# A graph network's last graph layer: 65-column matmuls become 32-column tiles, and in layer 0 the early sums move ahead of the bias rows

## The chip, the cores and the metric

The kernel runs on one core of one Trainium2 chip. The metric is the device time in microseconds of one execution. A core has a matrix engine (TensorE, with a queue for weight loads and one for matmuls), VectorE, ScalarE, GpSimd (POOL) and a queue for transfers (SyncE), which run side by side and wait for each other at semaphores. Each engine takes its own instructions in the order in which they stand, so one that waits holds up all that stand behind it on its engine.

## The reference, cut to what matters

The network has 3125 nodes of 256 features and 100,000 edges, and four layers. Each layer normalizes the rows, adds the results of a graph part and of a mixing part (attention without a softmax over pairs) to `x`, and then adds a feed-forward part with experts:

```python
edge_index = jnp.stack([src, dst])
xn = _layernorm(x, axis=-1)
x = x + _L0_gnn_ref(xn, edge_index, ...) + _L0_mix_ref(xn[None], ...)[0]
x = x + _L0_ffn_ref(_layernorm(x, axis=-1)[None], ...)[0]
...
xn = _layernorm(x, axis=-1)
x = x + _L3_gnn_ref(xn, edge_index, L3_gnn_W, L3_gnn_att_src, L3_gnn_att_dst) + _L3_mix_ref(xn[None], ...)[0]
x = x + _L3_ffn_ref(_layernorm(x, axis=-1)[None], ...)[0]
```

Two parts are touched by the change. The graph part of the last layer is graph attention with four heads of 64 channels:

```python
xp = (x @ W).reshape(n, 4, 64)
a_src = jnp.einsum('nhc,hc->nh', xp, att_src)
a_dst = jnp.einsum('nhc,hc->nh', xp, att_dst)
e = jax.nn.leaky_relu(a_src[src] + a_dst[dst], 0.2)
e_exp = jnp.exp(e - e_max[dst])
denom = jax.ops.segment_sum(e_exp, dst, num_segments=n)
alpha = e_exp / denom[dst]
out = jax.ops.segment_sum(alpha[:, :, None] * xp[src], dst, num_segments=n)   # then relu
```

The feed-forward part of layer 0 sends each node to two of 16 experts:

```python
topk_vals, topk_idx = jax.lax.top_k(x @ gate_w + gate_b, 2)
topk_w = jax.nn.softmax(topk_vals, axis=-1)
expert_out = relu(x @ w1 + b1) @ w2 + b2          # per expert
y = x + jnp.sum(topk_w[..., None] * sel, axis=2)  # sel: the two chosen outputs
return layernorm(y) * gamma + beta
```

Layer 2's graph part weights messages by `edge_weight`; for it the kernel needs sums of the edge weights by source node, which depend on no layer and are computed early.

## The kernel before, in words

**Layout.** Nodes lie as 25 blocks (`NB`) of 125 (`P`) rows: `self.x` and `self.xn` are [125, 25, 256], `self.xt` is the normalized matrix transposed. Work over nodes goes in seven `PIECES` of up to 500 columns (`PW`): six of 500 and one of 125. All matmuls named here are float32. `self.bank()` gives one of four rotating accumulators of the matrix engine's output memory (PSUM[...]); `evac` (L159) copies an accumulator out, on VectorE and ScalarE in turn.

**The order of work.** The program is traced in Python, and a scheduler places each engine's instructions at build time by priority, which follows the order of tracing, and by its own estimate of times. The code shapes it by the order in which it traces, by generators that yield their progress (`together`, L1905, always advances the one that is behind), by an edge that keeps instructions behind a given one (`issue_after`), and by the number of buffers of each tile.

**The last graph layer (`l3_gnn_mix`, L1837; `l3_dense`, L1915).** The attention over edges is done densely: the number of edges from source block b to target piece p is stored in DRAM as bf16 (`ctt_d`), and the exponential of the leaky relu is written as a product of a source factor and a target factor plus a relu. `xr` [125, 25, 4, 65] holds the features by source block and head with a 65th column of ones, so the same matmul that sums the messages also sums the weights (`denom`). The pieces are taken two by two (three groups of 1000 targets, then one of 125), the heads two by two, except in the last group, which does four at once. For each of these turns there are 25 steps, one a source block b:

- SyncE loads the adjacency rows `cs` (two transfers by `move`, three buffers);
- for each head of the turn ScalarE makes `t` (L1965), VectorE makes `z = (t + u) * cs` (L1968, three buffers), 125 x 1000;
- TensorE adds into one accumulator for each head and piece, with 65 columns of weights (L1971):

```python
nc.tensor.matmul(acc[h, k][:, :w], xr[:, b, k4, :], z[:, k * PW:k * PW + w],
                 start=(b == 0), stop=(b == NB - 1))
```

Four accumulators live through a turn. At its end they are evacuated into `at`, a part of `self.xn` that is free in this stage, transposed back by blocks of 125 targets (L1987), and `finish` (L1923) divides by the sum, applies the relu and adds to `x`: five small VectorE operations for each block. `target_rows` loads the target factors `rows` of the next group. In the same stage runs the mixing part by pieces (`l3_mix_by_pieces`, L2005), paced at 1.15 to 1.0, and behind every finished piece the router of the last feed-forward part (`follow` in `l3_ffn`), with its scatter of rows `bx_d` by POOL (L2255).

**Layer 0's feed-forward part (`l0_ffn`, L1050).** VectorE works out a slot for every node and choice; POOL scatters the rows of `self.xn` into DRAM by 50 indirect transfers (L1117). `add_rows` adds `beta` to `x` (L982), and `times_rows` (L285) adds the experts' second biases, weighted by the gates, onto `self.xn`, into which the experts' outputs are gathered later: for each piece a transpose of the gates (L291), an evacuation, and for each block a matmul (L297) and an addition on VectorE (L298). Since this addition writes a block of `self.xn` that the scatter reads, it waits for that block's two transfers. Then come the first quarter (`EARLY = 0.25`) of the sums of edge weights (`weights_by_source`, L509), kept behind the instruction `placed`, which makes the slots:

```python
with tc.issue_after(placed.ins):
    for part in sums:
        if part > EARLY:
            break
```

A group of these sums is five VectorE operations (L537, L539, three at L543, each with three buffers) and four bf16 matmuls (L545). After them the 26 expert tiles follow: load of the rows `xb`, transposes (L1156), copies `xbt` on VectorE (L1158), the first matmul (L261), relu, the second matmul (L1168), and a further share of the sums with each tile.

Of the kernel before, what the change touches and what calls it, by code (L numbers as in the profile page):

```python
# [12 lines left out]
F32 = mybir.dt.float32  # L13
# [4 lines left out]
AF = mybir.ActivationFunctionType  # L18
OP = mybir.AluOpType
# [4 lines left out]
N = 3125  # L24
D = 256
P = 125
NB = 25
# [10 lines left out]
PW = 500  # L38
# [52 lines left out]
def _tables():  # L91
# [12 lines left out]
    t[NT1 * 128:NT1 * 128 + NB, 0] = np.arange(NB) * P  # L104
    return np.ascontiguousarray(t.reshape(NT1 + 1, 128, 4).transpose(1, 2, 0))
EARLY = 0.25
PIECES = [(i, min(PW, N - i)) for i in range(0, N, PW)]


class Net:  # L110
    NE, TS = 16, 384
# [938 lines left out]
    def l0_ffn(self, fast=False):  # L1050

        nc, tc, a = self.nc, self.tc, self.a
        NE, TS, ST, NT, bx = self.NE, self.TS, self.TS // 128, self.NT, self.bx
        by = self.dram.tile([NT * TS, D], F32, name="b0y_d")
        with ExitStack() as s:
            sb = s.enter_context(self.pool("f0_sb"))
            wk = s.enter_context(self.pool("f0_wk", 2))
            b2 = sb.tile([NE, D], F32, name="b2")
            nc.scalar.dma_start(b2, a["L0_ffn_b2"])
            gamma = self.load_b(sb, "L0_ffn_gamma")  # L1060
            beta = self.load_b(sb, "L0_ffn_beta")
            g, w, i8 = self.top2(sb, None, NE, P, NB, self.greatest)
# [17 lines left out]
            for e in range(NE):  # L1080
                nc.vector.tensor_tensor_scan(run[:, :, e], self.ones[:, :NB], tot[:, :, e], 0.0,
                                             op0=OP.mult, op1=OP.add)
# [4 lines left out]
                                    op0=OP.mult)  # L1087
# [15 lines left out]
            own = sb.tile([1, NT], I32, name="own")  # L1103
# [11 lines left out]
            for b in range(NB):  # L1115
                for j in range(2):
                    st = nc.gpsimd.indirect_dma_start(  # L1117
                        out=bx, out_offset=bass.IndirectOffsetOnAxis(ap=slot[:, j, b:b + 1], axis=0),
                        in_=self.xn[:, b, :], in_offset=None, bounds_check=NT * TS - 1, oob_is_err=False)
                    tc.declare_no_dep(st.ins, group="slots", reason="each choice has a slot of its own")  # L1120
                    tc.add_to_no_dep_group("slots", st.ins)
            self.add_rows(beta)
            y = self.xn
            self.times_rows(sb, g, b2, NE, y, self.xn)
            with ExitStack() as s2:
                sums = None
                if fast:
                    sums = self.weights_by_source(s2.enter_context(self.pool("w_sb")),
                                                  s2.enter_context(self.pool("w_wk", 3)), self.bank())

                    with tc.issue_after(placed.ins):
                        for part in sums:
                            if part > EARLY:
                                break
                wk2 = s2.enter_context(self.pool("f0_t", 3))
                pl = s2.enter_context(self.pool("f0_ps", 4, space=PSUM))
                s2.enter_context(tc.manual_schedule(engines={mybir.EngineType.SP}))
# [4 lines left out]
                for i in range(NT):  # L1142
# [10 lines left out]
                    for h in range(HB):  # L1153
                        ps = bank()
# [5 lines left out]
                    for f in range(4):  # L1160
                        ps = bank()
# [675 lines left out]
    def l3_gnn_mix(self, before, arrivals):  # L1837
# [6 lines left out]
        with ExitStack() as s:  # L1844
# [9 lines left out]
            sb = s.enter_context(self.pool("g3_sb"))  # L1854
            wk = s.enter_context(self.pool("g3_wk", 2))
            pa = s.enter_context(self.pool("g3_ps", 1, space=PSUM))
            xr = sb.tile([P, NB, 4, 65], F32, name="xr")
            nc.gpsimd.memset(xr[:, :, :, 64:65], 1.0)
            al = sb.tile([P, NB, 8], F32, name="al")
            for b in range(NB):  # L1860
                ps = self.bank()
                self.mm_tok(ps[:P, :264], self.xt, b, wx)
                nc.vector.tensor_copy(xr[:, b, :, :64], ps[:P, :D].rearrange("p (h d) -> p h d", h=4))
                nc.scalar.copy(al[:, b, :], ps[:P, 256:264])
            m = sb.tile([P, 8], F32, name="m")
            nc.vector.tensor_reduce(m, al.rearrange("p b h -> p h b"), axis=AX.X, op=OP.max)
# [47 lines left out]

    def l3_dense(self, sb, wk, pa, xr, us, r_d):  # L1915

        nc = self.nc
        few = sb.tile([P, NB, 4], F32, name="few")
        free = self.xn.rearrange("p b d -> p (b d)")
        rows = free[:, :8 * PW].rearrange("p (h d) -> p h d", h=4)  # L1920
        at = free[:65, 8 * PW:12 * PW].rearrange("p (h d) -> p h d", h=2)

        def finish(b, h0, nh, acc):  # L1923

            nc.vector.tensor_scalar(few[:, b, h0:h0 + nh], acc[:, :, 64], 1e-20, None, op0=OP.is_lt)
            rd = wk.tile([P, 4], F32, name="rd")
            nc.vector.tensor_scalar(rd[:, :nh], acc[:, :, 64], 1e-20, None, op0=OP.max)
            nc.vector.reciprocal(rd[:, :nh], rd[:, :nh])
            t = wk.tile([P, 4, 64], F32, name="tf")
            nc.vector.tensor_mul(t[:, :nh], acc[:, :, :64], rd[:, :nh, None].to_broadcast([P, nh, 64]))  # L1930
            v = self.x[:, b, h0 * 64:(h0 + nh) * 64]
            nc.vector.scalar_tensor_tensor(v, t[:, :nh].rearrange("p h d -> p (h d)"), 0.0, v,
                                           op0=OP.max, op1=OP.add)

        def target_rows(i, h0):

            n = min(2 * PW, N - i)
            for h in (h0, h0 + 1):
                if n > 0:
                    self.move(nc.sync, rows[:P, h, :n], r_d[h, i:i + n].partition_broadcast(P))  # L1940

        done, there = 0, []
        for h0 in (0, 2):
            target_rows(0, h0)
        for p0 in range(0, len(PIECES), 2):
            pcs = PIECES[p0:p0 + 2]
            n = sum(w for _, w in pcs)
            hg = 4 if n < PW else 2
            for h0 in range(0, 4, hg):
                acc = {}  # L1950
                for h in range(hg):
                    for k in range(len(pcs)):
                        acc[h, k] = pa.tile([65, 512], F32, name=f"acc{h * len(pcs) + k}")
                for b in range(NB):
                    cs = wk.tile([P, 2, PW], BF, name="cs", bufs=3)
                    if len(pcs) == 2:
                        self.move(nc.sync, cs, self.ctt_d[p0:p0 + 2, :, b, :].rearrange("k p d -> p k d"))
                        c = cs.rearrange("p k d -> p (k d)")
                    else:
                        self.move(nc.sync, cs[:, 0, :n], self.ctt_d[p0, :, b, :n])  # L1960
                        c = cs[:, 0, :n]
                    for h in range(hg):
                        k4 = h0 + h
                        t = wk.tile([P, 2 * PW], F32, name="t5")
                        nc.scalar.activation(t[:, :n], rows[:, k4, :n], AF.Relu, bias=us[:, 2, b, k4:k4 + 1],  # L1965
                                             scale=us[:, 0, b, k4:k4 + 1])
                        z = wk.tile([P, 2 * PW], F32, name="z", bufs=3)
                        nc.vector.scalar_tensor_tensor(z[:, :n], t[:, :n], us[:, 1, b, k4:k4 + 1], c,  # L1968
                                                       op0=OP.add, op1=OP.mult)
                        for k, (i, w) in enumerate(pcs):  # L1970
                            nc.tensor.matmul(acc[h, k][:, :w], xr[:, b, k4, :], z[:, k * PW:k * PW + w],  # L1971
                                             start=(b == 0), stop=(b == NB - 1))
                        done += n
                    yield done / (NB * N * 4)
                    if b == 5:
                        for i in there:
                            self.arrive(i)
                        there = []
                if hg == 2:
                    target_rows(pcs[0][0] + 2 * PW, h0)  # L1980
                    for h in range(2):
                        for k, (i, w) in enumerate(pcs):
                            self.evac(at[:, h, k * PW:k * PW + w], acc[h, k][:, :w])
                    for j in range(n // P):
                        ps = self.bank()
                        for h in range(2):
                            nc.tensor.transpose(ps[:P, h * 65:(h + 1) * 65], at[:, h, j * P:(j + 1) * P],  # L1987
                                                self.ident[:65, :65])
                        finish(p0 * 4 + j, h0, 2, ps[:P, :130].rearrange("p (h c) -> p h c", h=2))
                        yield done / (NB * N * 4)  # L1990
                else:
                    for h in range(4):
                        self.evac(at[:, h // 2, h % 2 * P:(h % 2 + 1) * P], acc[h, 0][:, :P])
                    ps = self.bank()
                    for h in range(4):
                        nc.tensor.transpose(ps[:P, h * 65:(h + 1) * 65], at[:, h // 2, h % 2 * P:(h % 2 + 1) * P],
                                            self.ident[:65, :65])
                    finish(p0 * 4, 0, 4, ps[:P, :260].rearrange("p (h c) -> p h c", h=4))

            there = [i for i, w in pcs]  # L2000
        for i in there:
            self.arrive(i)
        nc.vector.tensor_reduce(self.viol[:P, 5:6], few.rearrange("p b h -> p (b h)"), axis=AX.X, op=OP.add)
# [421 lines left out]
```

## Time and profile before

| | |
|---|---|
| Time, median of 3 runs | 4813.85 us (4810.83 to 4815.78) |
| The profiled execution's own time | 4666.18 us |
| Its span | 4664.4 us |
| TensorE clock granted, mean | 0.869 |
| TensorE busy | 3722.3 us (80%) |
| VectorE busy | 2505.6 us (54%) |
| ScalarE busy | 1302.8 us (28%) |
| POOL busy | 1020.2 us (22%) |
| Dense loop of the last graph layer | about 3530 to 4395 us of the span |
| Slots, scatter and early sums of layer 0 | about 796 to 926 us |

The profile is of one execution, with 50,401 instructions; its own time is 147.7 us below the median of the timed runs. A group of instructions is given as source line, engine, operation, the tile it writes and those it reads, shape and count, then busy time, mean duration in ns, idle time of the engine just before them, and what ended that idle time. PE is TensorE's matmul queue and PEld its weight loads; DVE is VectorE, ACT ScalarE. Durations of matmuls overlap, since they are pipelined; the distance of their starts tells what one costs. A float32 matmul shows as two records, each with a weight load of its own.

### The profile page before, as it was taken

The numbers are of one execution on the slowest core, as the hardware profiler recorded it, in microseconds if no ns is written. First come the engines' busy times: TensorE is split into PE (matmuls) and PEld (weight loads), VectorE is DVE, ScalarE is ACT, GpSimd is POOL, SyncE is SP. The second block draws the span as 40 slices with busy tenths as digits, with TensorE's granted clock in tenths as the row PEclk, the third lists the DMA queues.
The fourth block names the chain that finished last, engine by engine and source line by source line (L and its number), as shares of the span: only waits on it lengthen the run. The fifth ranks groups of instructions, "written<-read, shape, count | busy, mean of one in ns | idle before, by whom it ended". The sixth has DMA issues, their size and how long they took to land. (4 is left out here: it accounts for less than half of the span.)

```text
span 4664.4 us, 50401 instructions
## 1 busy us (share of the span) xinstructions
PE 3722.3 (80%) x16695; PEld 2505.9 (54%) x16695; DVE 2505.6 (54%) x8604; ACT 1302.8 (28%) x2336; POOL 1020.2 (22%) x1041
## 2 busy tenths in 40 slices
PE   1887796499938799999656566766799999999698
PEld 0676695277724556555545455655464444444466
DVE  5877317544475526994322323444265666777544
ACT  1367100022213223323100000000155655555521
POOL 2000000400055000000577777775000000000011
PEclk9786896599959799999877777887899999999699
DMA  6244630244332000000333333334102222221232
GB/s 176 75 113 118 138 82 22 81 135 140 107 85 40 4 29 9 13 14 7 106 105 106 104 104 104 104 104 139 58 7 59 59 63 56 63 52 49 74 107 68
DMA packets 256035, 358.86 MB, mean 77 GB/s; under 512 B 62719, under 2 KB 199350, under 8 KB 255765
## 3 DMA queue, kind: packets, MB, share of 16 engines
q1 hardware_dynamic: 135900, 176.07, 13.1%
q0 software_dynamic: 62832, 126.93, 10.3%
q10 hardware_dynamic: 57033, 52.54, 4.2%
q8 instruction: 136, 2.23, 0.2%
q14 instruction: 134, 1.10, 0.1%
HBM read 268.73 MB, written 94.97 MB: 78 GB/s over the span
## 5 line engine op out<-in xcount | busy, mean ns | idle before, releaser
L1601 POOL DMA_INDIRECT hg<-hx_d,idx x782 | 743.3, 950 | 282.8 <-issue 214.2
L1617 PE MATMUL acc<-hg,to 128*125 128x256 f32 x2042 | 584.5, 449 | 197.9 <-DVE to L1612 192.8
L1617 PEld LDWEIGHTS acc<-hg,to 128*125 128x125 f32 x2042 | 455.4, 227 | 309.3 <-DVE to L1612 216.3
L1971 PE MATMUL acc<-z,xr 125*65 125x500 f32 (+1 forms) x1400 | 577.4, 556 | 14.3 <-DVE z L1968 13.0
L1965 ACT ACTIVATE t<-xn,us 125x1000 f32<-125x1000 f32 (+1 forms) x400 | 409.4, 1037 | 239.0 <-DVE z L1968 228.1
L1968 DVE SCALAR_TENSOR_TENSOR z<-t,us,cs 125x1000 f32<-125x1000 f32 (+1 forms) x400 | 409.3, 1028 | 115.5 <-PE acc L1971 92.6
L1971 PEld LDWEIGHTS acc<-z,xr 125*65 125x65 f32 x1400 | 188.9, 145 | 314.8 <-issue 265.5
L1605 DVE TENSOR_TENSOR kw<-hg,awt 128x8 f32<-128x8 f32 x98 | 16.4, 168 | 581.2 <-DMA hg<-hx_d,idx 513.2
L261 PE MATMUL ps<-xt,w 128*128 128x500 f32 (+1 forms) x672 | 269.0, 547 | 1.8 <-DMA w<-in_L_ffn_W_dram 1.8
L1612 DVE TENSOR_SCALAR to<-iota_w,rel_b,kw 128x125 f32<-128x125 f32 (+1 forms) x782 | 245.2, 383 | 35.6 <-PE acc L1617 28.7
L1536 DVE SCALAR_TENSOR_TENSOR junk<-iota_w,rel_b,lock 128x125 f32<-128x125 f32 (+1 forms) x782 | 248.1, 386 | 0.0
L2255 POOL DMA_INDIRECT bx_d<-row,slot x25 | 31.2, 1248 | 891.3 <-ACT t L1965 422.9
L589 PE MATMUL ps<-y,cb 125*125 125x256 bf16 x1875 | 214.7, 279 | 0.0
L589 PEld LDWEIGHTS <-cb 125*125 125x125 bf16 x1875 | 213.5, 141 | 0.1
L797 ACT ACTIVATE k<-k 125x128 f32<-125x128 f32 x50 | 15.9, 318 | 687.0 <-DVE k L796 686.9
L190 ACT ACTIVATE rstd_t<-rstd_t 125x4 f32<-125x4 f32 (+2 forms) x86 | 17.2, 203 | 645.8 <-DVE rstd_t L189 630.2
L255 PE MATMUL ps<-wo,h 128*125 128x256 f32 x800 | 187.7, 386 | 3.6 <-ACT h L1439 2.6
L243 PE MATMUL ps<-ident,xn 125*128 125x125 f32 x300 | 58.8, 347 | 159.8 <-DVE xn L209 159.7
L1445 DVE SCALAR_TENSOR_TENSOR x<-ps,lg,x 125x256 f32<-125x256 f32 x200 | 92.7, 480 | 173.6 <-PE ps L255 173.6
L261 PEld LDWEIGHTS ps<-xt,w 128*128 128x128 f32 x672 | 122.7, 193 | 114.7 <-issue 102.4
L261 PE MATMUL ps<-h,w 128*128 128x500 f32 (+1 forms) x448 | 179.5, 541 | 2.3 <-ACT h L1434 1.6
L255 PEld LDWEIGHTS ps<-wo,h 128*125 128x125 f32 x800 | 142.9, 187 | 65.9 <-ACT h L1439 43.7
(566 smaller groups left out, 6326.7 us busy)
## 6 DMA issues: line engine op xcount, KB each, us to landing
cs<-ctt_d SPq DMA_DIRECT2D x150, 218.8 KB
w<-in_L_ffn_w_dram SPq DMA_DIRECT2D x52, 512.0 KB
cnt_d<-cd SPq DMA_DIRECT2D x25, 683.6 KB
cb<-cnt_d SPq DMA_DIRECT2D x25, 683.6 KB
ctt_d<-ct ACTq DMA_DIRECT2D x6, 2734.4 KB
hg<-hx_d,idx POOLq DMA_INDIRECT x782, 2.8
b0x_d<-zero SPq DMA_DIRECT2D x1, 9984.0 KB
xb<-b0x_d SPq DMA_DIRECT2D x26, 384.0 KB
```

The lines of the kernel that those rows point to most:

```text
L243: self.nc.tensor.transpose(ps[:, j * P:(j + 1) * P], src[:, i // P + j, h * 128:(h + 1) * 128], self.ident[:P, :P])
L255: self.nc.tensor.matmul(ps, xt[:, h, b * P:(b + 1) * P], w[:, h, :], start=(h == 0), stop=(h == k - 1))
L261: self.nc.tensor.matmul(ps, w[:, h, :], xt[:, h, i:i + n], start=(h == 0), stop=(h == k - 1))
L589: nc.tensor.matmul(ps[:P, :D], cf[k][:, h * P:(h + 1) * P], y3[:, b0 + k, j, :], start=(k == 0 and j == 0), stop=(k == m - 1 and j == 2))
L1445: nc.vector.scalar_tensor_tensor(self.x[:, b, :], ps[:P, :D], g[:, b, e:e + 1], self.x[:, b, :], op0=OP.mult, op1=OP.add)
L1536: nc.vector.scalar_tensor_tensor(junk[:, :m * P], self.iota_w[:, :m * P], rel[:, c:c + 1], lock[:, b:b + m].rearrange("p b n -> p (b n)"), ...
L1601: nc.gpsimd.indirect_dma_start(out=hg[:, j, :], out_offset=None, in_=hx, in_offset=bass.IndirectOffsetOnAxis(ap=idx[:, c0 + j:c0 + j + 1], ...
L1612: nc.vector.tensor_scalar(to, self.iota_w[:, :nb * P], rel[:, c:c + 1], kw[:, j:j + 1], op0=OP.is_equal, op1=OP.mult)
L1617: nc.tensor.matmul(acc[k], to[:, (k - b) * P:(k - b + 1) * P], hg[:, j, :D], start=(c == first[k]), stop=(c == last[k]))
L1965: nc.scalar.activation(t[:, :n], rows[:, k4, :n], AF.Relu, bias=us[:, 2, b, k4:k4 + 1], scale=us[:, 0, b, k4:k4 + 1])
L1968: nc.vector.scalar_tensor_tensor(z[:, :n], t[:, :n], us[:, 1, b, k4:k4 + 1], c, op0=OP.add, op1=OP.mult)
L1971: nc.tensor.matmul(acc[h, k][:, :w], xr[:, b, k4, :], z[:, k * PW:k * PW + w], start=(b == 0), stop=(b == NB - 1))
```

## The change

It has two parts, which do not touch each other.

In `l3_dense`, `xr` loses its column of ones. A step's four 65-column matmuls become twelve of 32 columns: for each of the two `units` (a piece; in the last group a pair of heads) two heads with two halves of 32 channels each, written to the four column tiles (`tile_position=(0, q)`, q = 0, 32, 64, 96) of that unit's accumulator, and four more with 32 columns of ones, whose 32 equal result rows are the sums of the weights, for both units in a third accumulator. Three accumulators live through a turn, of four names taken in rotation. `z` has four buffers instead of three, and `t` lies in two fixed places of `self.xn`, where `at` lay. Each matmul is tied in order behind the one before it and behind both `z` of its step, with a raised priority; at every third step (`BURST`) the tie to the matmul before is kept and one is added to an instruction of other TensorE work that was the latest three bursts (`LAG`) earlier. The end of a turn evacuates three accumulators, transposes the sums once and the results by units, and works on up to four blocks at a time.

In `l0_ffn`, `add_rows` and `times_rows` are traced after the early sums instead of before them.

```diff
+BURST, LAG = 3, 3
...
-            self.add_rows(beta)
             y = self.xn
-            self.times_rows(sb, g, b2, NE, y, self.xn)
             with ExitStack() as s2:
...
                         for part in sums:
                             if part > EARLY:
                                 break
+                self.add_rows(beta)
+                self.times_rows(sb, g, b2, NE, y, self.xn)
                 wk2 = s2.enter_context(self.pool("f0_t", 3))
...
-            xr = sb.tile([P, NB, 4, 65], F32, name="xr")
-            nc.gpsimd.memset(xr[:, :, :, 64:65], 1.0)
+            xr = sb.tile([P, NB, 4, 64], F32, name="xr")
...
-                        for k, (i, w) in enumerate(pcs):
-                            nc.tensor.matmul(acc[h, k][:, :w], xr[:, b, k4, :], z[:, k * PW:k * PW + w],
-                                             start=(b == 0), stop=(b == NB - 1))
...
+                acc = [pa.tile([128, 512], F32, name=f"acc{(turn + j) % 4}") for j in range(3)]
...
+                        t = spare[h % 2]
...
+                        z = zs[h] = wk.tile([P, 2 * PW], F32, name="z", bufs=4)
...
+                    if steps % BURST == 0:
+                        marks.append(next((i for i in reversed(nc.cur_bb.bb.instructions)
+                                           if i.engine == mybir.EngineType.PE and i.name not in own), None))
+                        if len(marks) > LAG and marks[-1 - LAG] is not None:
+                            made.append(marks[-1 - LAG])
+                    steps += 1
+                    with self.tc.high_priority(600):
+                        for out, left, h0, j, k, w, q in (
+                                [(acc[u], xr[:, b, h0 + j, f:f + 32], h0, j, k, w, 64 * j + f)
+                                 for u, (h0, k, w) in enumerate(units) for j in range(2) for f in (0, 32)]
+                                + [(acc[2], self.ones[:P, :32], h0, j, k, w, 64 * u + 32 * j)
+                                   for u, (h0, k, w) in enumerate(units) for j in range(2)]):
+                            mm = nc.tensor.matmul(out[q:q + 32, :w], left, zs[h0 + j][:, k * PW:k * PW + w],
+                                                  start=(b == 0), stop=(b == NB - 1), tile_position=(0, q))
+                            for i in made:
+                                self.tc.add_manual_dep(mm.ins, i.name, row, reason="in one row")
+                            made = [mm.ins]
+                            own.add(mm.ins.name)
...
-                    for j in range(n // P):
-                        ps = self.bank()
-                        for h in range(2):
-                            nc.tensor.transpose(ps[:P, h * 65:(h + 1) * 65], at[:, h, j * P:(j + 1) * P],
-                                                self.ident[:65, :65])
-                        finish(p0 * 4 + j, h0, 2, ps[:P, :130].rearrange("p (h c) -> p h c", h=2))
...
+                finish(b0, pcs[0][1] // P, hs[0], 2 * len(hs), acc)
```

The new `finish`:

```python
        def finish(b, nb, h0, nh, acc):
            w, nu = nb * P, len(acc) - 1
            at = wk.tile([128, 3, PW], F32, name="at", bufs=1)
            for k in range(nu + 1):
                self.evac(at[:, k, :w], acc[k][:, :w])
            ps = self.bank()
            for j in range(nb):
                nc.tensor.transpose(ps[:P, j * 128:(j + 1) * 128], at[:, nu, j * P:(j + 1) * P], self.ident)
            sums = ps[:P, :nb * 128].rearrange("p (j q r) -> p j q r", j=nb, r=32)[:, :, :, 0]
            ...
            for k in range(nu):
                bk, hk = (b + 4 * k, h0) if nh == 2 else (b, 2 * k)
                ...
                for j in range(nb):
                    nc.tensor.transpose(ps[:P, j * 128:(j + 1) * 128], at[:, k, j * P:(j + 1) * P], self.ident)
                t = wk.tile([P, 4, 2, 64], F32, name="tf")
                nc.vector.tensor_mul(t[:, :nb], ...)
                ...
                nc.vector.scalar_tensor_tensor(v, t[:, :nb].rearrange("p j h d -> p j (h d)"), 0.0, v,
                                               op0=OP.max, op1=OP.add)
```

## The prediction

> **What bounds the kernel now.** I read three things in this order: the page's costliest groups, the busy time by stretch over the last graph layer, and the timeline there; then the timeline of layer 0 around its scatter. (The chain that ended last is followed back over only 6% of the span and says nothing of either place.) The groups of the page:
>
> ```profile
> L1971 PE MATMUL acc<-z,xr 125*65 125x500 f32 (+1 forms) x1400 | 577.4, 556 | 14.3 <-DVE z L1968 13.0
> L1965 ACT ACTIVATE t<-xn,us 125x1000 f32<-125x1000 f32 (+1 forms) x400 | 409.4, 1037 | 239.0 <-DVE z L1968 228.1
> L1968 DVE SCALAR_TENSOR_TENSOR z<-t,us,cs 125x1000 f32<-125x1000 f32 (+1 forms) x400 | 409.3, 1028 | 115.5 <-PE acc L1971 92.6
> ```
>
> TensorE idles 14.3 us ahead of its 1400 records, VectorE waits 92.6 us for TensorE and ScalarE 228.1 us for VectorE: the queue of waits ends at TensorE. The 700 float32 matmuls of the code are 1400 records, two to a matmul. Busy time of the stage's two parts (PE, PEld, DVE, ACT, POOL, then clock, DMA share and GB/s):
>
> ```profile
> 3530.00:4313.00 783.00, 770.94 (x2343) 340.66 (x2342) 544.57 (x1053) 460.55 (x514) 20.47 (x16) 0.99 0.21 57
> 4313.00:4395.00 82.00, 64.50 (x287) 42.86 (x285) 54.55 (x241) 53.96 (x117) 9.54 (x8) 0.69 0.12 26
> ```
>
> For 783 us TensorE is the bound (98%, granted clock 0.99) with VectorE at 70%. In the last 82 us, the 125-wide group, it isn't. The timeline of TensorE gives the true price of a record:
>
> ```profile
> 3699.51 8.55 PE L1971 MATMUL acc<-z,xr 125*65 125x500 f32 x20
> 3707.89 1.97 PE L1321 MATMUL ps<-bd,q_e 128*125 128x132 f32 x16
> ```
>
> Twenty starts in 8.38 us: 0.419 us apart. The mean of all, from their starts, is 0.416; I use 0.4175, so a matmul of 500 columns costs 0.835 us. A step of the loop (one source block, two heads, two pieces) is 4 of them, 3.34 us, against VectorE's 2 x 1.25 = 2.5 us and ScalarE's 2 x 1.22 = 2.44 us. 150 such steps are 501 us of the 783; about 282 us are the mix and the router.
>
> In layer 0:
>
> ```profile
> 808.71 3.04 POOL L1117 DMA_INDIRECT b0x_d<-xn,slot  x1 [32.71 <-DVE slot L1114]
> 815.96 0.42 DVE L298 TENSOR_TENSOR xn<-ps,xn 125x256 f32<-125x256 f32 x1 [5.31 <-DMA b0x_d<-xn,slot]
> 889.47 0.42 DVE L298 TENSOR_TENSOR xn<-ps,xn 125x256 f32<-125x256 f32 x1 [1.83 <-DMA b0x_d<-xn,slot]
> 892.92 0.47 PE L1156 MATMUL pl<-ident,xb 128*128 128x128 f32 x1 [1.02 <-DMA xb<-b0x_d]
> 926.19 0.56 DVE L1158 COPY xbt<-pl 128x384 f32<-128x384 f32 x1
> 926.80 1.65 PE L261 MATMUL pl<-xbt,w 128*128 128x384 f32 x2
> ```
>
> The 25 additions of L298 each wait for two scatters, 54 us in all, and the early sums (L537 to L545) stand between and behind them. The first expert's rows are there at 892.9, but its matmuls begin at 926.8, because VectorE does sums until 926.2.
>
> **What the Trainium skill says.** *TensorE: Matmul & The Clock Gate*, "Measured speedup vs the span model": three 32-column tiles of 512 columns ran 2.38 times as fast as one after the other. The same page, "The mechanism": tiles overlap, but matmuls start and end strictly in program order. *TensorEngine Tiling (Array Packing)*, "Key Properties": tiles are independent, and a change of tiling mode drains the engine. No column tile is in the trace of before, so none of this is confirmed there. *SBUF — State Buffer*, "Summary: rules for kernel authors": descriptor generation on POOL starves while VectorE runs in a fast mode. The trace agrees in part: the scatter beside 1.95 us of VectorE work took 3.04 us, the median is 1.19.
>
> **Part 1: the dense loop (500-wide, 783 us).** Removed: 600 matmuls x 0.835 = 501.0 us. Added: 12 matmuls of 32 columns a step, 1800 in all, as 450 rows of four, each row on the four column tiles. The row's price is the unknown.
> - Floor: four tiles together, 0.835 us; 450 x 0.835 = 376 us.
> - By the skill's ratio (2.38 of 3, an estimate): 0.835 / 0.793 = 1.05 us; 473 us.
> - Ceiling that I take seriously: each matmul is two records on the same tile. If the second record of a tile holds up the next tile's first, only neighbours overlap and a row is 4 x 0.4175 = 1.67 us; 751 us.
>
> I take 0.87: the floor and a little for the staggered starts, because the weight loads of before (138 ns) are hidden in a spacing of 0.416, and the tiles are stated to be independent. 450 x 0.87 = 391.5, so **-109.5 us**.
>
> *Changes of mode.* In the changed program's order on TensorE the 1800 stand in 69 runs (23 of 36, the rest from 2 to 180), so 138 changes. A record lasts 582 ns at a spacing of 417, so a drain is at most about 0.165 us: 0 to 23 us; I take the half, **+11**.
>
> *The end of a turn.* 96 transposes whose starts are 184 ns apart (17.6 us) go; 6 turns x 12 = 72 come, at the 113 ns of the mix's transposes (7.9 us): **-9.7** on TensorE. On VectorE 48 times five small operations (0.142+0.147+0.157+0.291+0.292 = 1.03 us, 49 us) become 6 turns of about 3.3 us: 29 us less, off the path. The evacuations fall from four to three a turn, the loads of the adjacency rows stay at two a step.
>
> *Waiting for z.* TensorE's step falls to 2.61 us, next to VectorE's 2.5 and ScalarE's 2.44. z has four buffers, so VectorE is at most two steps ahead; a run of three steps needs one made during the run. VectorE has 544.6 - 373.7 (its z) - 29 = 142 us of other work in this stretch; whatever falls inside a run stops TensorE's queue, with the mix behind it. Before, 3.34 - 2.5 = 0.84 us a step covered that; this cover goes. At least 0 us, at most about half of the 142; I take a quarter, **+35**.
>
> Sum of part 1: -109.5 + 11 - 9.7 + 35 = **-73.2 us**. VectorE's 516 us are still below the 710 left.
>
> **Part 2: the 125-wide group (82 us).** ScalarE's 14 activations in 6.38 us are 0.456 each, 1.82 us a step; TensorE's three rows of two records at about 0.105 are 0.63 us. Hidden behind ScalarE: **0**. In the pairs case a step would be 12 x 0.21 = 2.5 us: +17.
>
> **Part 3: layer 0.** The early sums now stand ahead. In the new order 96 of their matmuls (24 groups of four) precede the first expert's transposes, which wait for its rows. TensorE's queue stops there, and after three more groups (three buffers) VectorE too: 27 of the 48 groups run in the scatter's window. The other 21 follow at 892.9, at 0.82 us each (the timeline repeats them every 0.82): 17.5 us, so the first copy is at about 911 and not 926: -15. With VectorE dense beside POOL for some 30 us the scatter is held up: 0 to 10 us, I take +5. The additions of L298 now stand in the first expert: 25 matmuls x 2 records x 0.215 (the spacing of 256-column records) = 10.7 us, and 21 transposes x 0.13 = 2.7 us, once under the scatter, now on the path: +13.4. Together **+3** (-20 to +18). The window is given up to one work instead of another.
>
> **Sum.** -73.2 + 0 + 3 = -70.2 us of the profiled execution's 4666.2 (span 4664.4, 1.8 us around it). The median shown is 4813.85, 1.0316 times as long; I know no cause for that and scale: -72.4, **4741 us**.
>
> **Rivals.**
> *Pairs (slower).* Program order makes a tile's two records hold up the next tile. For it: two records a matmul, and the skill's strict order. Against: the skill's independent tiles. 751 - 501 = +250, +11 - 9.7, +17 in the tail, +3: +272, scaled +280: **5094 us**. It decides from a row of about 1.07 us, where (501 + 9.7 - 11 - 15 - 3)/450 is reached.
> *The skill's ratio.* Row 1.05 us: -28.5 + 11 - 9.7 + 15 (fewer waits for z) + 3 = -9: **4804 us**, at the edge of no change; so the change wouldn't do what it says.
> *VectorE takes over.* Rows are fast, but TensorE waits for z the full 71 us: -109.5 + 11 - 9.7 + 71 + 3 = -34: **4779 us**. For it: 2.61 against 2.5 us a step; against: 516 of 710 us.
>
> **How the numbers follow.** Main case 0.57 (its own range 4640 to 4790), VectorE 0.12, the skill's ratio 0.09, pairs 0.18, something between ratio and pairs (weight loads that show, say) 0.04. Of the ratio case a third each is faster, the same and slower. Within 0.2% (9.6 us, about what a measurement of this kernel can tell from no change) is 0.04 with rounding; faster 0.57 + 0.12 + 0.03 = 0.72; slower 0.18 + 0.04 + 0.02 = 0.24. The floor of the row with no drain and no wait for z gives -125 - 10, and with layer 0's best -20 it is -155, scaled -160: low end 4640 with a little left out. The high end of 4880 takes in the ratio case and half of what lies between; the pairs case stays outside.
>
> **What would show it.** Starts of the 32-column records: four tiles near each other and 0.87 us from row to row (main), 0.417 us from each record to the next tile's (pairs). The 783 us stretch at about 710; VectorE's wait for acc near nothing, TensorE's wait for z from 13 to some 50 us. In layer 0, the first copy of xbt near 911 to 916, scatters somewhat above 1.19 us, and about 13 us of L298's matmuls inside the first expert. I am wrong if rows take over 1.07 us, or if a fall in the stretch doesn't reach the end.

## The result and the profile after

The changed kernel takes 4866.59 us (median of 4 runs, 4857.26 to 4872.12), the kernel before on the same chip 4812.34 us (4808.0 to 4815.78): ratio 1.0108, interval 1.0086 to 1.013. It is 54 us slower, where 72 us less were forecast.

The profiled execution after took 4857.26 us, its span is 4855.5. One thing has to be set aside before the two traces are compared: the gather of layer 2 (`hg`), which neither part touches, runs from 2244.7 to 3231.9 us in the trace of before (987 us) and from 2273.8 to 3408.1 in that of after (1134 us). In the traces kept here it goes with the chip: all runs below with a before of about 4668 us have the short gather, those with about 4800 us a long one (1116 to 1134 us). No trace shows the kernel before itself with the long gather, but the difference of 147 us is the size of the gap of 148 us between the profile of before and its median, which the prediction could not explain; so its scaling by 1.0316 had no ground (it moved 2 us). Below, stages other than this one are compared, and ratios only with runs of before on the same chip.

The groups of the page that answer to the three of before (columns: line, engine, operation, tiles and shapes, count, then busy time, mean ns, idle time before and its releaser):

```profile
L1986 DVE SCALAR_TENSOR_TENSOR z<-xn,us,cs 125x1000 f32<-125x1000 f32 (+1 forms) x400 | 400.2, 1027 | 134.5 <-PE acc L2002 84.2
L1983 ACT ACTIVATE xn<-xn,us 125x1000 f32<-125x1000 f32 (+1 forms) x400 | 405.4, 1037 | 186.3 <-DVE z L1986 176.0
...
L2002 PE MATMUL acc<-z,xr 125*32 125x500 f32 (+1 forms) x2800 | 379.6, 561 | 20.5 <-DVE z L1986 15.5
...
L2002 PE MATMUL acc<-z,ones 125*32 125x500 f32 (+1 forms) x1400 | 223.2, 550 | 0.0
```

TensorE still waits little for z: 15.5 us in place of 13.0. And VectorE still waits 84 us for TensorE to release a z buffer, where 92.6 stood before. So TensorE's queue still holds VectorE up, and not the other way round. The busy time by stretch, from the first to the last 500-wide record and then the 125-wide group (columns as in the prediction: length, busy PE, PEld, DVE, ACT, POOL, clock, DMA share, GB/s):

```profile
3711.40:4507.50 796.10, 717.07 (x4721) 313.02 (x4720) 528.21 (x896) 455.23 (x508) 20.78 (x16) 0.94 0.22 57
4507.50:4586.70 79.20, 62.43 (x666) 36.16 (x660) 48.15 (x205) 48.02 (x109) 9.58 (x8) 0.70 0.11 25
```

The same cut of before gives 785.1 us with TensorE busy 773.0 at a clock of 0.99, and 76.8 us. So the main stretch is 11 us longer, not 73 shorter, and TensorE stands idle for 79 us of it instead of 12. The rows themselves did what was hoped:

```profile
3765.20 1.88 PE L2002 MATMUL acc<-z,xr 125*32 125x500 f32 x16
3766.90 1.02 PE L2002 MATMUL acc<-z,ones 125*32 125x500 f32 x8
3767.74 1.86 PE L2002 MATMUL acc<-z,xr 125*32 125x500 f32 x16
```

Twenty-four records, a step, in 2.54 us; record by record, four tiles start 6.7 ns apart, and the next four 0.419 us after the first. A row of four matmuls costs 0.838 us, what one alone had cost.

Where TensorE stands idle, the timeline shows at the end of a piece of the mix:

```profile
4053.58 1.99 PE L256 MATMUL ps<-L_mix_W,hid 128*125 128x256 f32 x8 [0.53 <-DVE np_st L2087]
...
4058.89 1.23 DVE L2069 TENSOR_TENSOR o<-o,L_mix_g 125x1024 f32<-125x1024 f32 x1
...
4061.41 1.22 DVE L2072 TENSOR_TENSOR x<-x,o 125x1024 f32<-125x1024 f32 x1
...
4065.11 1.38 DVE L210 TENSOR_SCALAR row<-x,ln_mv,ln_rs 125x256 f32<-125x256 f32 x4
...
4065.58 0.68 PE L2230 MATMUL ps<-ident,row 125*128 125x125 f32 x2 [10.00 <-DVE row L210]
...
4074.49 0.19 DVE L2247 TENSOR_TENSOR hot<-iota_w,ix 125x32 f32<-125x32 f32 x1
...
4074.83 0.60 PE L2251 MATMUL ps<-hot,before 125*125 125x32 f32 x2 [3.26 <-DVE hot L2247]
...
4075.78 1.06 PE L2002 MATMUL acc<-z,xr 125*32 125x500 f32 x4
```

The mix's last matmuls, two normalizations on VectorE, the router's transposes, the softmax and the ranks hang on each other, and from 4053 to 4075.78 no dense row stands between them. Two steps of rows were ready all this time, for VectorE had filled the four z buffers by 4043.49:

```profile
4041.06 2.43 DVE L1986 SCALAR_TENSOR_TENSOR z<-xn,us,cs 125x1000 f32<-125x1000 f32 x2 [0.30 <-PE acc L2002]
...
4079.85 2.43 DVE L1986 SCALAR_TENSOR_TENSOR z<-xn,us,cs 125x1000 f32<-125x1000 f32 x2 [2.06 <-PE acc L2002]
```

It made no other z until 4079.85. So the rows did not miss their inputs; they stood behind the chain in TensorE's queue. The same stretches in pieces of 5 us, at their worst:

```profile
4060.00:4065.00 5.00, 0.00 (x0) 0.00 (x0) 4.59 (x13) 1.25 (x2) 0.00 (x0) 0.50 0.10 29
...
4070.00:4075.00 5.00, 1.74 (x10) 1.67 (x9) 2.96 (x22) 0.64 (x2) 0.00 (x0) 0.50 0.00 0
```

The granted clock falls to 0.50 with the idle time, so what follows is slow as well. *TensorE: Matmul & The Clock Gate*, "What's actually happening", of the Trainium skill says that the clock is halved after an idle window of about 3.4 us; ten idle microseconds here agree.

In layer 0:

```profile
820.79 21.92 POOL L1118 DMA_INDIRECT b0x_d<-xn,slot  x1 [0.30 <-issue]
843.02 1.19 POOL L1118 DMA_INDIRECT b0x_d<-xn,slot  x1 [0.30 <-issue]
...
916.13 1.11 PE L1157 MATMUL pl<-ident,xb 128*128 128x128 f32 x4 [75.74 <-DMA xb<-b0x_d]
...
917.54 0.43 DVE L538 TENSOR_TENSOR lo<-i,key 128x512 bf16<-128x512 bf16 x1 [75.89 <-PE ps L546]
...
936.51 0.54 DVE L1159 COPY xbt<-pl 128x384 f32<-128x384 f32 x1
```

One transfer of the scatter took 21.92 us instead of 1.19. TensorE and VectorE stopped, as the prediction had said, but for 76 us, until the rows were there at 916.1 and not at 892.9; and the first copy stands at 936.5, not at 911. The experts of layer 0 end 27.4 us later (the gathers `yg` behind them start at 1305.8, not 1278.4).

### The profile page after: what moved, and what is told of

It reads as the page before. It is cut to its first block, busy times and chain, and to the rows that moved or that the text cites. A ratio compares the mean times of both kernels' runs of the same rounds, so it can differ in the third digit from the quotient of the medians.

```text
span 4855.5 us, 55684 instructions
## 1 busy us (share of the span) xinstructions
PE 3687.4 (76%) x19470; PEld 2470.4 (51%) x19470; DVE 2493.8 (51%) x8419; ACT 1296.7 (27%) x2332; POOL 1040.3 (21%) x1040
## 5 line engine op out<-in xcount | busy, mean ns | idle before, releaser
L1618 PE MATMUL acc<-hg,to 128*125 128x256 f32 x2042 | 600.2, 450 | 292.0 <-issue 138.0
L1986 DVE SCALAR_TENSOR_TENSOR z<-xn,us,cs 125x1000 f32<-125x1000 f32 (+1 forms) x400 | 400.2, 1027 | 134.5 <-PE acc L2002 84.2
L1983 ACT ACTIVATE xn<-xn,us 125x1000 f32<-125x1000 f32 (+1 forms) x400 | 405.4, 1037 | 186.3 <-DVE z L1986 176.0
L2002 PE MATMUL acc<-z,xr 125*32 125x500 f32 (+1 forms) x2800 | 379.6, 561 | 20.5 <-DVE z L1986 15.5
L2002 PE MATMUL acc<-z,ones 125*32 125x500 f32 (+1 forms) x1400 | 223.2, 550 | 0.0
L2002 PEld LDWEIGHTS acc<-z,xr 125*32 125x32 f32 x2800 | 103.9, 113 | 220.3 <-issue 134.4
```

What stands on the lines that cost most here:

```text
L1618: nc.tensor.matmul(acc[k], to[:, (k - b) * P:(k - b + 1) * P], hg[:, j, :D], start=(c == first[k]), stop=(c == last[k]))
L1983: nc.scalar.activation(t[:, :n], rows[:P, h, :n], AF.Relu, bias=us[:, 2, b, h:h + 1], scale=us[:, 0, b, h:h + 1])
L1986: made.append(nc.vector.scalar_tensor_tensor(z[:, :n], t[:, :n], us[:, 1, b, h:h + 1], c, op0=OP.add, op1=OP.mult).ins)
L2002: mm = nc.tensor.matmul(out[q:q + 32, :w], left, zs[h0 + j][:, k * PW:k * PW + w], start=(b == 0), stop=(b == NB - 1), tile_position=(0, q))
```

## The experiments

TensorE's time in the main stretch is split by the starts of its records: work on the dense rows, other work (mix and router), idle. "Runs" counts the runs of dense rows in the stretch. The parts can miss the stretch by 1 us from rounding.

| kernel | ratio to before (95%) | stretch, us | dense | other | idle | runs |
|---|---|---|---|---|---|---|
| before | 1 | 785 | 508 | 265 | 12 | 142 |
| after (both parts) | 1.0108 (1.0086 to 1.013) | 796 | 419 | 298 | 79 | 69 |
| l3_only | 1.0028 (1.0017 to 1.004) | 792 | 418 | 296 | 78 | 69 |
| l3_b1l3 | 1.006 (1.0043 to 1.0077) | 794 | 428 | 294 | 71 | 107 |
| l3_nolag | 1.0161 (1.0142 to 1.0179) | 766 | 488 | 239 | 39 | 162 |
| l3_ties | 1.0171 (1.0142 to 1.0199) | 868 | 507 | 296 | 64 | 46 |
| l3_noprio | 0.9976 (0.9966 to 0.9987) | 761 | 445 | 286 | 30 | 127 |
| l3_plain | 0.9962 (0.9954 to 0.997) | 752 | 444 | 279 | 29 | 125 |
| l3_atom | 0.9872 (0.9856 to 0.9889) | 717 | 422 | 272 | 22 | 101 |

The theories: (1) the order that the change gives the rows, runs of three steps taken early, leaves mix and router uncovered; (2) the tiles themselves cost, at each change between column tiles and full matmuls; (3) z is late.

**One part alone.** `l0_only` has the moved bias rows, `l3_only` the column tiles.

> Part 3 alone: the early sums ahead of the bias rows in layer 0, the last graph layer as before. My reading of the two traces: one scatter transfer is stretched to some 22 us while VectorE makes the sums, and 13 us of bias rows move onto the path, so about 27 us slower than before (ratio 1.005 to 1.007), the scatter ends near 908 us, the first copy of xbt is near 936. Rival: the later start of layer 1 seen in the changed kernel comes from elsewhere, then this is within 5 us of before.

> Parts 1 and 2 alone: column tiles in the last graph layer, layer 0 as before. If the loss of the stage is its own: 10 to 27 us slower than before (ratio 1.002 to 1.006), TensorE idle for some 80 us in the dense stretch, dense records about 0.84 us from row to row. Rival: the two parts disturb each other; then this is no slower than before, or 20 us and more faster.

`l0_only`: 4704.4 us, ratio 1.0077 (1.0056 to 1.0098), 36 us slower and so somewhat more than expected. Scatter until 909.8, first copy 936.2: as in the changed kernel. `l3_only`: 4682.17, ratio 1.0028, 14 us, idle 78 us. The parts add up (50 of 54 us), so the rival, that they disturb each other, falls. In the trace of `l0_only` the experts of layer 0 end 46 us later than before (`yg` at 1324.3), where the changed kernel has 27; its last graph layer gives some 4 us back. The 19 us lie between the first and the fifth copy (64.8 us instead of 46.0), where the same work runs at another clock. First the stretch in `l0_only`, then in the changed kernel:

```profile
950.00:970.00 20.00, 20.00 (x47) 11.22 (x46) 6.12 (x16) 2.31 (x4) 0.00 (x0) 0.50 0.08 26
```

```profile
950.00:970.00 20.00, 19.66 (x105) 13.86 (x104) 10.80 (x33) 3.04 (x6) 0.00 (x0) 1.00 0.19 51
```

Both are busy throughout, but `l0_only` does 47 matmul records where the other does 105; it stayed at half clock until about 983, the changed kernel until about 945. Before had full clock from 930. Why the clock came back so differently stays open.

**The ties loosened, two ways.**

```diff
-BURST, LAG = 3, 3
+BURST, LAG = 3, 1000000      # l3_nolag
+BURST, LAG = 1, 3            # l3_b1l3
```

> As l3_only, without the tie of every third step to other TensorE work of three bursts earlier; rows stay in order behind each other. Theory 1 (the ties leave no dense row between the dependent instructions of mix and router, so their latency stands on TensorE): TensorE's idle time in the stretch falls from some 80 to 10 to 40 us, the stage is 40 to 90 us shorter than in l3_only, ratio to before 0.983 to 0.995. Theory 2 (each change between column tiles and full matmuls is dear; runs of dense rows go from 77 to 183): 10 to 40 us slower than l3_only. Theory 3 (VectorE's z is the bound): the same time as l3_only, within 5 us.

> As l3_only, with BURST 1 in place of 3: one step of rows at a time, each tied to other TensorE work of three steps earlier; 113 runs of dense rows instead of 77. Theory 1: rows lie between more of the dependent instructions, so 15 to 60 us faster than l3_only. Theory 2: 5 to 20 us slower than l3_only. Theory 3: within 5 us of it.

Both missed what theory 1 said: 64 and 15 us slower than `l3_only`. The 15 lie in the range of theory 2, but not where it put them: the stretch is only 2 us longer, and 10 us are lost in the 125-wide group (89.5 us instead of 79.1). In `l3_b1l3` the idle time hardly fell (71 us): one-step runs at the raised priority are still gone before the waits come. In `l3_nolag` it fell to 39 us, in a stretch that holds less of the mix, and the stretch is 26 us shorter; but the dense work rose by 70, and the 125-wide group behind it took 157 us instead of 79: the rows overtook the mix and left it alone at the end. Why the dense work rose, its timeline shows:

```profile
3834.82 1.02 PE L2002 MATMUL acc<-z,ones 125*32 125x500 f32 x2
3835.77 1.11 PE L2064 MATMUL ps<-ot,L_mix_W 128*128 128x500 f32 x2
3836.81 1.03 PE L2002 MATMUL acc<-z,ones 125*32 125x500 f32 x2
```

A single matmul of 32 columns, two records, between full ones. It takes the time of a whole row. 82 of the 162 runs are such single matmuls; rounded up to whole rows the runs hold 539 rows instead of 450. 539 x 0.838 = 452, and the changes of mode are seen in the starts: the full matmul after a dense record comes 0.513 us after it, where 0.419 is normal, and a row after a 132-column record 0.206 instead of 0.112. That is 0.09 each, some 0.2 us a run with the slower first row, 32 us for 162 runs. By the split above, 0.12 us a run of this counts as dense work, 20 us, and the rest as other work: 472 of the 488 us. The other 16 lie in the long runs, some 9 of them in records at a lowered clock. So theory 2 is right that changes of mode cost, and the cost is small in the changed kernel: 69 runs, 14 us.

**The order alone, and the tiles alone.** `l3_ties` is the kernel before, with 65-column matmuls, in the change's order; `l3_plain` has the column tiles without it.

```diff
 # l3_ties, on the kernel before (z with four buffers)
+if steps % BURST == 0:
+    ...
+        made.append(marks[-1 - LAG])
+with self.tc.high_priority(600):
...
+        for i2 in made:
+            self.tc.add_manual_dep(mm.ins, i2.name, row, reason="in one row")
 # l3_plain, on l3_only
-zs, made = {}, made[-1:]
+zs, made = {}, []
...
-    with self.tc.high_priority(600):
```

(`l3_plain` also has no `LAG` tie.)

> The kernel before with its 65-column matmuls, but in the order of the change: chained, three steps in a run, every third step tied to other TensorE work of three bursts earlier, raised priority, four z buffers. Theory 1 (the order costs, not the tiles: it leaves mix and router without cover): TensorE idles some 60 to 100 us in the dense stretch instead of 12, and the kernel is 50 to 110 us slower than before (ratio 1.011 to 1.024). Theory 2 (the column tiles cost: changes of mode, slower full matmuls beside them): within 10 us of before. Theory 3 (z is late): within 10 us of before, since TensorE needs 3.34 us a step here.

> Column tiles in the last graph layer without the change's order: a step's twelve matmuls behind each other and behind its z, no tie from step to step, none to other work, no raised priority; 133 runs of dense rows, many of them parts of a step. Layer 0 as before. Theory 1: TensorE's idle time in the stretch falls from 78 to 10 to 35 us; with some 28 us for changes of mode the kernel is 20 to 70 us faster than before (ratio 0.985 to 0.996). Theory 2: slower than l3_only by 10 to 40 us (twice the changes of mode). Theory 3: runs of one step wait for z inside the run; within 10 us of l3_only.

`l3_ties`: 4885.65 against 4801.08 us, +85. Not one column tile is in it, and its stretch is 83 us longer: theories 2 and 3 said within 10. Its stretch, and the router's transposes in it:

```profile
3674.10:4541.90 867.80, 803.60 (x2337) 360.15 (x2336) 554.57 (x1055) 464.72 (x515) 20.10 (x16) 0.94 0.19 52
```

```profile
L2228 PE MATMUL ps<-ident,row 125*128 125x125 f32 x32 | 7.6, 354 | 20.5 <-DVE row L210 20.5
L2249 PE MATMUL ps<-hot,before 125*125 125x32 f32 x8 | 2.4, 396 | 13.0 <-DVE hot L2245 13.0
```

The changed kernel has 20.5 and 15.3 us in these places; the kernel before:

```profile
L2211 PE MATMUL ps<-ident,row 125*128 125x125 f32 x32 | 6.1, 299 | 2.7 <-DVE row L209 2.7
L2232 PE MATMUL ps<-hot,before 125*125 125x32 f32 x8 | 1.5, 265 | 0.0
```

The dense work is unchanged at 507 us; the 83 are 52 of idle time and 31 of other work, which is the same work done slower: the clock is 0.94 instead of 0.99, and a router transpose takes 354 ns on average instead of 299. `l3_plain`: ratio 0.9962, 20 us faster than before, idle 29. This is the lower edge of theory 1's range; what it leaves, dense work of 444 us, is again broken rows: 76 of 125 runs are not whole rows.

**How much waiting there is to cover.**

```diff
+if b in (0, NB - 1):
     zs, made = {}, made[-1:]
     ...                        # activations, z and matmuls of the step
```

> As l3_only, but 23 of the 25 steps of each turn are left out (activations, z and matmuls; the adjacency rows are still loaded), so the graph sums of the last layer aren't made: what mix and router take in this place by themselves. Theory 1: TensorE works about 300 us in it and waits 100 to 250 us for VectorE and ScalarE in the chain of mix and router; the loop takes 420 to 560 us. Theory 2: the other work is the fuller for the tiles: about 280 us of work, idle under 60 us, the loop takes about 340 us.

The loop took 425.6 us, TensorE busy 338.6 and idle 87 of it (within theory 1's range of the loop; the wait below its range of 100 to 250). The router's transposes in its first 329 us, half of those of the loop:

```profile
L2231 PE MATMUL ps<-ident,row 125*128 125x125 f32 x16 | 4.3, 375 | 10.0 <-DVE row L210 10.0
```

Ten us of waiting for sixteen, where the changed kernel has 20.5 for 32. So in the changed kernel these waits stand as bare as if there were no dense rows at all. (The whole run took 14306 us: with the sums left out the kernel repeats its work by another way, as 1758 gathers instead of 782 show. Only the loop is read.)

**Which of the ties.** `l3_noprio` keeps all ties and drops only the raised priority.

```diff
-with self.tc.high_priority(600):
```

> As l3_only with all its ties (steps chained, every third step behind other TensorE work of three bursts earlier), but without the raised priority of the rows: 135 runs of dense rows instead of 77. If the raised priority takes the rows away from the waits of mix and router: TensorE's idle time in the main stretch falls from 78 to 15 to 45 us, the time is that of l3_plain within 10 us (ratio to before 0.994 to 0.998). If the ties do it: idle stays above 60 us, ratio 1.000 to 1.006.

4788.8 against 4799.56 us, ratio 0.9976; idle 30 us, almost the 29 of `l3_plain`, which has neither. So it is enough to drop the priority; the ties to other work that remain uncover little. The likely reason, argued and not shown, is that at a raised priority a run goes as soon as its z and its tie allow, and none is left when the chain waits.

**Whole steps as filler.** `l3_atom` is `l3_plain` with the raised priority for the second to twelfth matmul of a step alone, so that a step goes whole once it has begun:

```diff
+if made[0] is not mm.ins and not own & {m.name for m in made}:
+    rest.enter_context(self.tc.high_priority(600))
 made = [mm.ins]
```

> As l3_plain (column tiles, no tie from step to step or to other work), but the second to twelfth matmul of a step have the raised priority, so that a step once begun is issued whole: 109 runs of dense rows, nearly all of 12 or a multiple, instead of 133, many of them parts of a step. Layer 0 as before. Theory 1 with the remainder of l3_plain put down to broken rows: dense work in the main stretch falls from 445 to 410 to 430 us, idle stays at 15 to 40 us, 10 to 35 us faster than l3_plain, ratio to before 0.989 to 0.995. If broken rows don't matter: within 5 us of l3_plain. If it is the whole runs that uncover mix and router: idle rises above 50 us and the time is that of before or above.

4608.13 against 4668.05 us: ratio 0.9872 (0.9856 to 0.9889), 60 us faster than before, and better than either kernel of this case. Against `l3_plain` that is 40 us, more than the 10 to 35 expected; dense work (422 us) and idle time (22 us) are as expected. Its stretch:

```profile
3532.40:4249.70 717.30, 695.21 (x4713) 284.58 (x4712) 515.78 (x895) 451.37 (x506) 21.46 (x16) 0.99 0.23 63
```

```profile
L2234 PE MATMUL ps<-ident,row 125*128 125x125 f32 x32 | 6.0, 283 | 1.8 <-DVE row L210 1.8
L2255 PE MATMUL ps<-hot,before 125*125 125x32 f32 x8 | 1.6, 284 | 1.1 <-DVE hot L2251 1.1
```

The waits of the router are covered again, the clock is 0.99, and only 14 of 101 runs are broken. The stretch of 717 us is near the "about 710" of the prediction, but not by its terms: that had 402 us of dense rows and 35 of waiting for z, this has 422 and 22 of idle time in all.

**The scatter.** Which property of VectorE's work stretches the transfer?

```diff
 # l0_f32: early groups compare float32 copies
-nc.vector.tensor_tensor(lo, i4, key[...], op=OP.is_equal)
+nc.vector.tensor_tensor(lo, i4f, keyf[...], op=OP.is_equal)
 # l0_psum: one operand from PSUM
+ip = self.bank().rearrange("p (j q) -> p j q", q=4)
+nc.vector.tensor_copy(ip, i4)
+nc.vector.tensor_tensor(lo, ip, key[...], op=OP.is_equal)   # oh goes to PSUM too
```

> As l0_only, but the comparisons of the early sums read float32 tiles instead of bf16 (copied once), so that VectorE isn't in its fast mode for most of them; the products stay. Starved scatter (the sums' fast operations keep POOL from its work): the longest scatter transfer falls from 21.9 us to under 4 us, the scatter ends near 890 instead of 910 us, 10 to 20 us faster than l0_only. Rival (the long transfer waits for something else, a queue or a DMA): one transfer still takes some 20 us, time within 5 us of l0_only.

> As l0_only, but the early sums' comparisons read their counting tile from PSUM, and the product of each group reads the comparison from PSUM, so that every operation of the groups has one operand in SBUF instead of two. Two SBUF operands are the cause: no scatter transfer above 5 us after the first few, the scatter ends at 888 to 893 us. Any dense VectorE work is the cause: one transfer still takes 14 us or more and ends about 1 us after VectorE stops. Its time tells nothing of the transfer alone, since float32 comparisons are slower: 4 to 40 us above before.

`l0_f32`: the comparisons are twice as slow (0.60 us from start to start instead of 0.34), so the fast mode is gone, and yet:

```profile
823.95 18.50 POOL L1123 DMA_INDIRECT b0x_d<-xn,slot  x1 [0.30 <-issue]
...
841.12 0.26 DVE L545 TENSOR_TENSOR ohf<-i4f,keyf 128x100 f32<-128x100 f32 x1
842.75 1.20 POOL L1123 DMA_INDIRECT b0x_d<-xn,slot  x1 [0.30 <-issue]
```

The transfer ends at 842.45, 1.07 us after VectorE's last operation (841.38); in `l0_only` too it ended 1.07 us after (842.48 and 841.41). The expected cure failed: the scatter ends at 906.8, and with slower sums the kernel is not faster than `l0_only` but at 1.01 (1.0072 to 1.0128). `l0_psum`, its sums as dense:

```profile
820.44 0.59 DVE L550 TENSOR_TENSOR ow<-ps,part 128x100 bf16<-128x100 f32 x3
820.93 1.19 POOL L1124 DMA_INDIRECT b0x_d<-xn,slot  x1 [0.30 <-issue]
820.95 0.26 DVE L546 TENSOR_TENSOR ps<-ps,key 128x100 f32<-128x100 f32 x1
```

Every transfer beside these sums takes 1.19 us (VectorE has one gap, of 0.28 us, from 812 to 835), and the scatter ends at 886.5, as before the change. So dense operations with two operands in SBUF hold the scatter up, and the fast mode isn't needed. *SBUF — State Buffer*, "Summary: rules for kernel authors", of the Trainium skill has this in the row on running VectorE beside GpSimd: if an operation of VectorE has two SBUF inputs and that of GpSimd reads SBUF, the later of the two waits for the first to end. The trace agrees, but the wait here, 21.9 and 18.5 us, did not end with one operation; it lasted until VectorE's operations stopped. The prediction had used another row of that table, on the fast mode. The total of `l0_psum`, 4703.11 us (ratio 1.0072), stays that of `l0_only`: the sums left over behind the scatter are slower (first copy at 939.0), and the bias rows are still in the first expert, at half clock until about 955.

## Why the prediction was wrong

- *Price of a row*: right. 0.838 us; 0.87 was taken. The rivals "pairs" (1.67) and "the skill's ratio" (1.05) fall.
- *Changes of mode*: right in size, +11 forecast; 69 runs at 0.2 us are 14. That the half of the upper bound came so near was luck: it was a guess.
- *Dense rows as a sum*: -109.5 + 11 = -98.5 forecast, -89 measured (508 to 419). The cheaper row is eaten up: 28 of the 69 runs end in half a row, so they hold 465 rows, 390 us; 8 us are changes of mode, some 9 us come from records at a lowered clock, and some 6 from short waits for z that do not show as idle time.
- *End of a turn*: -9.7 forecast. The transposes of the stretch went from 82 records with 9.5 us to 60 with 8.5: -1. Their starts are 0.116 us apart before, not 0.184 (and 72 x 0.113 is 8.1, not 7.9).
- *Waiting for z, +35*: **this step failed**. It measured +3, or some 9 with the short waits above. It asked what in a run waits for VectorE, and never what waited between the runs: the kernel before filled the waits of mix and router with dense matmuls, and the order in the new program (69 runs, the largest group of three steps) was read only as a count of mode changes. The 282 us of mix and router were carried over, but for the end of a turn, as if they cost the same in any order: a term put at nothing without a reason. Uncovered, those waits cost +64 us of idle time and +33 us of slower other work. The four terms give -89 + 3 + 64 + 33 = +11, the measured change of the stretch. The sign that the prediction had named, VectorE's wait for TensorE near nothing, failed with it: 84 us.
- *Part 2*: right, +2 us against 0.
- *Layer 0, +3*: that VectorE holds the scatter up was right, though not by its fast mode; **the term "scatter held up" was mis-sized**: +5 (0 to 10) forecast. The first rows came 23 us later, 2 of which were there before the scatter began: +21. The first copy then came 20.4 us behind the rows instead of 33.3, -13 (-15 forecast), and the bias rows in the first expert cost +17 (13.4 forecast; 46.0 instead of 29.0 us between the first and the fifth copy, with 16.6 us of their matmuls and transposes, in part at half clock). Sum +25, and 2 from before the scatter.
- *Sum*: +11 + 2 + 27 = 40 us explained in the traces, +54 measured (interval some 41 to 63); the two parts alone gave 14 and 36. The 14 us between 40 and 54 stay open: the trace of before has the short gather of layer 2 and that of after the long one, so the two can't be subtracted as wholes.
- *Rival "VectorE takes over"*: it named TensorE waiting, but for z; that wait stayed at 6 us in the stretch. No rival had the wait that decided.

That the lost cover, and not the tiles, is the cause is shown by `l3_ties` (the loss without tiles), `l3_noprio` (less idle time with the priority alone dropped) and `l3_atom` (the gain with another order). The fourth buffer of z, which `l3_ties` has too, was not tried apart. How the 33 us of slower other work divide between the lower clock and other causes stays open.

## What to carry to other kernels

Matmuls that depend on little are not only work, they are the filler for chains that wait; before grouping them or raising their priority, find what they cover and read the new order for what stands between two dependent instructions. Let them begin at their natural priority and keep only a small unit together, here one step of three rows (a single row was not tried). Before VectorE work is moved beside transfers issued by GpSimd, count its operands in SBUF.

## What was unexpected of the hardware

- Four column tiles run fully together: starts 6.7 ns apart, a row of four float32 matmuls of 500 columns in 0.838 us, each with its two records. A lone one takes the same.
- A single indirect transfer was held for as long as VectorE's operations with two SBUF operands followed each other without a gap: 21.9 us, ended 1.07 us after the last.
- The clock after a long wait came back at different times in the same code: after 76 us of idle time TensorE stayed at half clock for some 30 us in the changed kernel and for some 65 in `l0_only`, in one profiled execution of each.
